# A two-layer graph network on one core: 64 more edge tiles counted, one-source compares for the one-hots, and fewer signals from TensorE

## The chip, the cores and the metric

The kernel runs on one core of a Trainium2 chip. Its time is the device time of one execution in microseconds; the number compared is the median of several runs. Engines are named as in the profile: PE is TensorE (matrix products), PEld its weight loads, DVE is VectorE, ACT is ScalarE, POOL is GpSimd, SP is SyncE, which here only starts transfers. Each engine works through its own list of instructions in order; an instruction can wait for a semaphore that another engine raises.

## The reference, cut to what matters

There are 12,500 nodes with 32 features and 200,000 edges, sorted by their destination `dst`. Two layers follow each other, each added to `x`:

```python
h = relu(layernorm(x))
# layer 0: sum of the neighbours' rows
agg = segment_sum((h * rsqrt(max(out_deg, 1)))[src], dst, N)
x = x + (agg * rsqrt(max(in_deg, 1))) @ W + b
...
# layer 1: a small network on every edge, then the mean over a node's edges
msg = concat([h[dst], h[src] - h[dst]])             # h = relu(layernorm(x)) again
m = relu(relu(relu(msg @ W1 + b1) @ W2 + b2) @ W3 + b3) @ W4 + b4
x = x + segment_sum(m, dst, N) / max(count, 1)
```

So the rows of `src` have to be fetched by index (a gather) or counted, and the rows of `dst` are summed over a sorted list.

## The kernel before, in words

The edges are cut into tiles of 128 (1563 of them) and chunks of four tiles (391). Sums over destinations are products with one-hot matrices: a tile's rows are multiplied with a matrix that has a 1 where an edge belongs to a node of a window of 128, and windows move on by 32 nodes a chunk. One gather instruction of POOL (L211, in `gather`) fetches 128 rows by index; a chunk takes four of them.

**Stage 0** (0 to about 475 us): the layer norm, the degrees (one-hots L325, products L342), tables of rows written to DRAM, and the gathers of the first 64 chunks ("early").

**Stage 1**, the first layer (about 480 to 1960 us), has three kinds of chunks.
- The 64 early chunks are in SBUF already. `scale_rows` looks up each edge's factor (`sturned` L659, products L677, `mask` L684) and sums them (L706). One is started every `LATER` = 3 steps.
- The chunks 64 to 267 (up to `DIR` = 268) are gathered: four gathers `rows`, and two steps later `sum_rows` with four products into `ps_late` (L641).
- The last `ND` = 491 tiles, from chunk 268 on, are counted and not gathered. For each tile a matrix `oh` (edges by 98 × 13 columns: block of 128 nodes, place in the tile's window of 13 destinations) and a one-hot `lo` of the low seven bits of the source are made. Their product (`count_two`: two matmuls of 429 columns in a PSUM tile of two banks; `count_third`: one of 416; L789) says how often a source feeds a destination. ACT copies the counts to SBUF in two instructions (L791). After eight tiles, `multiply` multiplies the counts with a table of all nodes' rows, which stays in SBUF: 98 products of 104 columns (L738), spread over five of the next eight tiles, then a transpose and a placing product (L752, L757).

The one-hots `oh` are made for two tiles at once by a two-source compare (L726, 2574 columns): `keys` holds an edge's key for each third of the blocks, spread over the columns, against the column numbers `count_h`. It works two pairs ahead.

The order is written out by hand. A step of the loop at L807 issues the four gathers of one chunk, then about 2.4 count tiles (`slots`, L819), and with the first of these the one-hots of the next chunk, the running `scale_rows`, and the sums of the chunk gathered two steps before. `count_edges` is a generator, and one `next` is one tile.

**Stage 2**, the second layer (about 2010 to 4340 us): `NPAIR` = 196 steps, each for a pair of chunks. A step issues eight gathers `gj` (six buffers), the loads `ai` (L882) and `row` (L885) on SP for the step three later, and the stages of four pairs, at lags of 1, 3, 4 and 5 steps:
- `first` (L904): transposes of `gj` and one-hot products with `ai` into `p1`; ACT makes `h1` (L920).
- `second` (L923): four products with `w2s` (L930) into `p2`; ACT makes `h2` (L932).
- `third` (L934): sixteen products (L940) into `p3`; DVE makes `h3` (L943).
- `fourth` (L947): sixteen products of `h3` with the one-hots `hot` (made on DVE, L584) into the sums `ps`; every other step `add_messages` adds them to the accumulators (L558, L560) and now and then starts `finish_nodes` (the last product, L869, and the output).

`turn` makes the one-hots `turned` for the next pair's `first` (DVE, L892). The order of a step in before is gathers, loads, `finish_nodes`, then first, second, third, fourth as they were put in the list, each with the ACT or DVE instruction that reads its product right behind it. Each stage's products end with a signal of PE to that reader; PSUM buffers come from pools in turn (`p1` and `p3` two, `p2` one).

Of the kernel before, what the change touches and what calls it, by code (L numbers as in the profile page):

```python
# [8 lines left out]
F32 = mybir.dt.float32  # L9
BF16 = mybir.dt.bfloat16  # L10
F16 = mybir.dt.float16
# [46 lines left out]
LATER = 3  # L58
# [6 lines left out]
DIR = 268  # L65
# [19 lines left out]
def gnn_kernel(  # L85
# [59 lines left out]
    keys = early.tile([P, 3, ND + 1], F16, name="keys")  # L145
# [64 lines left out]
    def gather(tile_ap, table, col):  # L210
        nc.gpsimd.indirect_dma_start(  # L211
            out=tile_ap, out_offset=None, in_=table,
            in_offset=bass.IndirectOffsetOnAxis(ap=col, axis=0))
# [72 lines left out]
    with tc.tile_pool(name="deg", bufs=3) as hp, tc.tile_pool(  # L286
# [105 lines left out]
        base_ps = pp.tile([P, ND], F32, name="base_ps")  # L392
        nc.tensor.matmul(base_ps, ones, base_f, start=True, stop=True)
        drel = hp.tile([P, ND], F32, name="drel", bufs=1)
        nc.vector.tensor_tensor(drel, dst_i[:, DIR * TPC : NTR], base_ps, op=OP.subtract)
        nc.vector.tensor_reduce(bounds[:, 0:1], drel, AX.X, OP.min)
        nc.vector.tensor_reduce(bounds[:, 1:2], drel, AX.X, OP.max)
        key = hp.tile([P, ND], F32, name="key", bufs=1)
        nc.vector.scalar_tensor_tensor(
            key, hl[:, 0, DIR * TPC : NTR], float(WD), drel, op0=OP.mult, op1=OP.add)  # L400
        nc.vector.memset(keys[:, :, ND:], 0.0)
        for k in range(3):
            nc.vector.tensor_scalar(keys[:, k, :ND], key, float(-KW * k), None, op0=OP.add)
# [194 lines left out]
    with tc.tile_pool(name="e0", bufs=8) as sp, tc.tile_pool(name="nu", bufs=1) as np_, tc.tile_pool(  # L598
# [53 lines left out]
        def scale_rows(g):  # L652
# [4 lines left out]
            yield  # L657
            turned = sp.tile([PART, CHUNK], BF16, name="sturned", bufs=2)
            nc.vector.tensor_scalar(turned, row, part_s[:PART], None, op0=OP.is_equal)  # L659
            h = rows_early[:, g, :, :D]  # L660
            if g < RAW:
# [3 lines left out]
                nc.vector.tensor_sub(h, h, m[:, :, None].to_broadcast([P, TPC, D]))  # L665
                square = sp.tile([P, TPC, D], F32, name="raw_sq", bufs=2)
# [21 lines left out]
            if g < RAW:  # L688
# [4 lines left out]
                scaled, h, 0.0, w[:, :, None].to_broadcast([P, TPC, D]), op0=OP.max, op1=OP.mult)  # L693
            rows = sp.tile([P, TPC, D3], BF16, name="rows_scaled", bufs=2)
# [7 lines left out]
            yield  # L702

            total = ps[:D3, 1]
            for t in range(TPC):
                nc.tensor.matmul(  # L706
                    total, rows[:, t, :], hot[:, t // 2, :, t % 2], start=(t == 0), stop=(t == TPC - 1))
            adds.append((g, total))
# [8 lines left out]
        los, onehots, counts = {}, {}, {}  # L717
        LATE = (TD - 3, TD - 2)

        def onehots_of(i):  # L720

            if i % TPC == 0:
                c = DIR * TPC + i
                los[i // TPC] = one_hots(dp, hl[:, 1, c : c + TPC], P, "lo", 3)
            onehots[i // 2] = oh = dp.tile([P, 3, KW, 2], BF16, name="oh", bufs=4)
            nc.vector.tensor_tensor(  # L726
                oh, keys[:, :, i : i + 2][:, :, None, :].to_broadcast([P, 3, KW, 2]),
                count_h[:, None, :, :].to_broadcast([P, 3, KW, 2]), op=OP.is_equal)
# [35 lines left out]
        def count_edges():  # L764
# [3 lines left out]
            onehots_of(0)  # L768
            onehots_of(2)
            for i in range(ND):  # L770
# [7 lines left out]
                if i % 2 == 0 and i + 4 < ND:  # L778
                    onehots_of(i + 4)
                oh, lo = onehots[i // 2], los[i // TPC]  # L780
                if t not in LATE:
                    next(before, None)

                for ranges, name in ((THIRDS[:2], "two"), (THIRDS[2:], "third")):
                    k0, a, b = THIRDS.index(ranges[0]), ranges[0][0], ranges[-1][1]
                    ps = pp.tile([P, len(ranges), 512], F32, name=f"count_{name}")
                    w = (b - a) // len(ranges) * WD
                    for k in range(len(ranges)):
                        nc.tensor.matmul(  # L789
                            ps[:, k, :w], lo[:, i % TPC // 2, :, i % 2], oh[:, k0 + k, :w, i % 2], start=True, stop=True)  # L790
                    nc.scalar.activation(  # L791
                        counts[g][:, t, a:b, :].rearrange("p (k h) d -> p k (h d)", k=len(ranges)), ps[:, :, :w], AF.Copy)
# [14 lines left out]
        for m in range(EARLY, DIR + LAG + 1):  # L807
# [3 lines left out]

            while adds:
                early, total = adds.pop()
                sums.add(slice(0, D3), STEP * early, total)
                added([early])
            if EARLY <= m - LAG - 1:
                add_rows(m - LAG - 1)
            i = m - EARLY
            slots = range(stages * i // steps, stages * (i + 1) // steps)  # L819
            for slot in slots:  # L820
# [335 lines left out]
```

## Time and profile before

| | |
|---|---|
| median of 10 runs | 4344.57 us (4329.93 to 4361.16) |
| the profiled execution | 4349.91 us |
| its span, first to last instruction | 4347.8 us (2.1 us lie around it) |
| mean granted clock of TensorE | 0.737 |

The costliest groups, as busy time and mean of one:

| what | how many | mean ns | busy us |
|---|---|---|---|
| POOL gathers `gj`, stage 2 (L211) | 1563 | 946 | 1478.2 |
| POOL gathers `rows`, stage 1 (L211) | 816 | 946 | 772.2 |
| PE third's products (L940) | 3128 | 322 | 513.8 |
| PE products with the table (L738) | 6076 | 226 | 424.2 |
| PE count products, two (L789) | 982 | 417 | 324.0 |
| ACT copies of the counts, two (L791) | 491 | 886 | 435.2 |
| ACT copies of the counts, third (L791) | 491 | 513 | 251.8 |
| DVE one-hots of two count tiles (L726) | 246 | 1488 | 365.6 |

The durations of PE's products overlap, since products are pipelined. The views used below are the page with the shares of the span, the same by stretch of the span ("windows"), the groups of instructions by line, the list of waits (engine and instruction, what ended the wait, total us, number, longest) and the order of time (start, duration, engine, line, output and inputs, and in brackets the engine's idle time before it with what ended it: "remote" is a releaser that the profile can't name, "issue" is idle time in which the engine waited for nothing that the profile shows).

### The profile page before, as it was taken

The page shows a single profiled execution, that of the slowest core. Times are in us where ns is not written, and L with a number is a line of the kernel's source. Part 1 is how long each engine was busy: PE and PEld are TensorE (multiplying, and loading weights), DVE is VectorE, ACT ScalarE, POOL GpSimd, SP SyncE. Part 2 cuts the span into 40 slices and gives each one's busy share as a digit, 9 for nine tenths or more (in the row PEclk, how much of TensorE's full clock was granted, in tenths as well). Part 3 has the DMA queues.
Part 4 walks back from the last instruction along what each step waited for, and adds up shares of the span by engine and source line. Part 5 has one row for each costly group of instructions (what it writes and reads, how often), then busy time and mean ns, then how long its engine had stood idle before and what let it go on. Part 6 is the DMA issues. An engine that isn't in the chain of part 4 may idle for free.

```text
span 4347.8 us, 54122 instructions
## 1 busy us (share of the span) xinstructions
PE 2909.2 (67%) x20860; PEld 1948.3 (45%) x20860; DVE 1821.0 (42%) x4113; ACT 1108.1 (25%) x2034; POOL 2501.6 (58%) x2655
## 2 busy tenths in 40 slices
PE   2444276777777777763667676777777777777777
PEld 2333154555555555551344444444444444444445
DVE  6555465666556566541222232222323222232224
ACT  0000244455544455430111111111111111111112
POOL 6555355555555555445566666666666666666663
PEclk9555588888888888865676777767767777667778
DMA  3000211111111111111222222222222222222221
GB/s 77 11 11 10 60 20 19 24 22 27 24 24 24 20 25 30 21 37 36 45 50 51 51 50 52 51 51 51 50 51 53 51 51 51 50 50 54 47 54 32
DMA packets 234664, 170.64 MB, mean 39 GB/s; under 512 B 156040, under 2 KB 182888, under 8 KB 234400
## 3 DMA queue, kind: packets, MB, share of 16 engines
q0 software_dynamic: 84320, 75.96, 11.0%
q1 hardware_dynamic: 131338, 85.26, 7.3%
q10 hardware_dynamic: 18742, 5.89, 0.7%
q8 instruction: 168, 2.75, 0.3%
q14 instruction: 96, 0.79, 0.1%
HBM read 153.98 MB, written 12.92 MB: 38 GB/s over the span
## 4 chain that ended last, share of the span: by engine, by line
PE 41%; another core or an unknown queue 19%; issue 16%; DVE 9%; ACT 8%; POOL 6%; DMA 1%; DVEq 0%; ACTq 0%; POOLq 0%
PE p L940 8%; PE p L930 6%; ACT count L791 6%; POOL gj L211 5%; PE count_two L789 4%; PE ps L958 4%; PE st L738 4%; PE p L916 4%; PE p L912 3%; DVE lo L325 2%; POOL rows L211 2%; PE count_third L789 2%; DVE hi L325 1%; PE ps_late L641 1%
## 5 line engine op out<-in xcount | busy, mean ns | idle before, releaser
L211 POOL DMA_INDIRECT gj<-tab_j,src_j x1563 | 1478.2, 946 | 904.3 <-issue 417.3
L211 POOL DMA_INDIRECT rows<-tab_hn,src_j x816 | 772.2, 946 | 747.4 <-PE ps_late L641 386.2
L940 PE MATMUL p<-w3s,h 128*128 128x64 f32 x3128 | 513.8, 322 | 177.6 <-issue 131.3
L943 DVE TENSOR_TENSOR h<-p,b3n 128x512 f32<-128x512 f32 x196 | 135.3, 690 | 1110.2 <-remote 491.1
L791 ACT ACTIVATE count<-count_two 128x858 bf16<-128x858 f32 x491 | 435.2, 886 | 624.9 <-remote 263.4
L940 PEld LDWEIGHTS p<-w3s,h 128*128 128x128 f32 x3128 | 473.3, 234 | 224.0 <-issue 166.7
L932 ACT ACTIVATE h<-p,b2s 128x1024 f32<-128x1024 f32 x196 | 218.0, 1112 | 1216.1 <-remote 546.9
L789 PE MATMUL count_two<-oh,lo 128*128 128x429 bf16 x982 | 324.0, 417 | 293.8 <-ACT count L791 239.6
L738 PE MATMUL st<-count,table 128*128 128x104 bf16 (+1 forms) x6076 | 424.2, 226 | 115.4 <-issue 72.0
L738 PEld LDWEIGHTS <-table 128*128 128x128 bf16 x6076 | 380.7, 105 | 180.3 <-issue 138.1
L930 PE MATMUL p<-h,w2s 64*128 64x512 f32 x782 | 383.1, 866 | 106.0 <-issue 87.9
L726 DVE TENSOR_TENSOR oh<-keys,kept 128x2574 bf16<-128x2574 f16 x246 | 365.6, 1488 | 54.3 <-PE ps_late L641 19.9
L958 PEld LDWEIGHTS ps<-hot,h 128*64 128x64 f32 x3126 | 233.9, 170 | 303.0 <-issue 152.4
L958 PE MATMUL ps<-hot,h 128*64 128x128 f32 x3126 | 269.7, 326 | 130.3 <-DVE h L943 129.4
L789 PEld LDWEIGHTS <-lo 128*128 128x128 bf16 x1473 | 150.8, 110 | 417.2 <-issue 368.9
L916 PE MATMUL p<-turned,ai 128*64 128x512 f32 x782 | 309.2, 837 | 20.0 <-issue 19.5
L342 PE MATMUL deg_ps<-hi,lo 128*128 128x98 bf16 x1563 | 182.8, 269 | 197.6 <-issue 132.5
L211 POOL DMA_INDIRECT rows_early<-tab_h,src_j x224 | 211.8, 946 | 157.9 <-DVE src_j L334 90.9
L912 PE MATMUL p<-ident,gj 128*128 128x128 f32 x784 | 195.2, 365 | 113.9 <-issue 113.4
L560 DVE TENSOR_TENSOR acc<-acc,ps 64x64 f32<-64x64 f32 (+1 forms) x198 | 44.6, 225 | 536.1 <-PE p L912 259.6
L892 DVE TENSOR_TENSOR turned<-row,kept 128x512 f32<-128x512 f16 x391 | 249.6, 679 | 33.8 <-remote 15.8
L791 ACT ACTIVATE count<-count_third 128x416 bf16<-128x416 f32 x491 | 251.8, 513 | 5.7 <-PE count_two L789 3.8
(201 smaller groups left out, 2918.1 us busy)
## 6 DMA issues: line engine op xcount, KB each, us to landing
row<-rel_row SPq DMA_DIRECT2D x195, 256.0 KB
gj<-tab_j,src_j POOLq DMA_INDIRECT x1563
rows<-tab_hn,src_j POOLq DMA_INDIRECT x816
ai<-tab_i SPq DMA_DIRECT2D x195, 64.0 KB
srow<-hi_row SPq DMA_DIRECT2D x64, 98.0 KB
rows_early<-tab_h,src_j POOLq DMA_INDIRECT x224
tab_j<-nu_aij SPq DMA_DIRECT2D x23, 128.0 KB
tab_i<-nu_aij SPq DMA_DIRECT2D x23, 128.0 KB
```

Of the source, the lines that this page charges most:

```text
L211: nc.gpsimd.indirect_dma_start(out=tile_ap, out_offset=None, in_=table, in_offset=bass.IndirectOffsetOnAxis(ap=col, axis=0))
L726: nc.vector.tensor_tensor(oh, keys[:, :, i : i + 2][:, :, None, :].to_broadcast([P, 3, KW, 2]), count_h[:, None, :, :].to_broadcast([P, 3, ...
L738: nc.tensor.matmul(ps[:, : tiles * WD], table[:, h, :], c[:, :tiles, h, :], start=(h == 0), stop=(h == PART - 1))
L789: nc.tensor.matmul(ps[:, k, :w], lo[:, i % TPC // 2, :, i % 2], oh[:, k0 + k, :w, i % 2], start=True, stop=True)
L791: nc.scalar.activation(counts[g][:, t, a:b, :].rearrange("p (k h) d -> p k (h d)", k=len(ranges)), ps[:, :, :w], AF.Copy)
L892: nc.vector.tensor_tensor(turned, v["row"][:, k], part_f.to_broadcast([P, CHUNK]), op=OP.is_equal)
L912: nc.tensor.matmul(p1[:, t, :], v["gj"][:, t].rearrange("p k c -> p (k c)"), ident, is_transpose=True, start=(t == 0), stop=False, skip_gr ...
L916: nc.tensor.matmul(p1[k * HID : (k + 1) * HID].rearrange("p t e -> p (t e)"), v["ai"][:, k], v["turned"][k], start=False, stop=True, skip_ ...
L930: nc.tensor.matmul(p2[:, k], w2s[s, :], v["h1"][s, :], start=True, stop=True)
L932: nc.scalar.activation(h2[:, :n], p2[:, :n], AF.Relu, bias=b2s)
L940: nc.tensor.matmul(p3[:, k * TPC + t, :], v["h2"][:, k, t * P : (t + 1) * P], w3s, start=True, stop=True)
L958: nc.tensor.matmul(ps[k * HID : (k + 1) * HID, o : o + W], v["h3"][:, k * TPC + t, :], v["hot"][k][:, t, :], start=(i == 0 and t == 0), st ...
```

## The change

It has three parts.

**Less is gathered, more is counted.** `DIR` goes from 268 to 252, so that 188 chunks are gathered in stage 1 (before 204), and 555 tiles are counted (before 491). A step has about three count tiles instead of 2.4. `scale_rows` is started every eighth slot and no more every third step, with more `yield`s in it, and the sums and the running generators are advanced in every slot.

**How a tile is counted.** The one-hots are made for one tile at a time, four tiles ahead, in seven buffers, by a one-source compare (`tensor_scalar`) of the column numbers `count_s` with the edge's key, which is a scalar of each partition. The two PSUM tiles of the counts are made once. The third product is split in 8 and 408 columns. Both of ACT's copies are made to wait for the tile's last product, so that PE raises its semaphore once a tile and no more twice.

**The order of stage 2.** In a step PE does fourth, third and first, then the products of `finish_nodes`, then second; the lags are 1, 2, 4 and 6. All instructions that read products (`past_first`, `past_second`, ...) come after second, in the lists of ACT and DVE. `ends[step]` is second's last product; h3's instruction, the gathers (of the step five later) and the `ai` loads are made to wait for it (`behind`), and with the in-order lists this stands for the signals of the other stages. PSUM buffers are fixed tiles.

The instructions that the programs hold, before and after: signals of PE in stage 2's stages 881 and about 206; signals of PE by count products 982 and 555, by all of stage 1 1588 and 1226; products by the count tiles 1473 and 2220; products with the table 6076 and 6860; gathers of `rows` 816 and 752.

```diff
-LATER = 3
+LATER = 8
-DIR = 268
+DIR = 252
...
-    keys = early.tile([P, 3, ND + 1], F16, name="keys")
+    key = early.tile([P, ND], F32, name="key")
+    count_s = early.tile([P, 3 * KW], F16, name="count_s")
...
         for k in range(3):
-            nc.vector.tensor_scalar(keys[:, k, :ND], key, float(-KW * k), None, op0=OP.add)
+            nc.vector.tensor_scalar(
+                count_s[:, KW * k : KW * (k + 1)], count_h[:, :, 0], float(KW * k), None, op0=OP.add)
...
+        count_ps = {name: pp.tile([P, n, 512], F32, name=f"count_{name}") for name, n in (("two", 2), ("third", 1))}
+        FIRST = 8
+        AHEAD_OH = 4
...
-            onehots[i // 2] = oh = dp.tile([P, 3, KW, 2], BF16, name="oh", bufs=4)
-            nc.vector.tensor_tensor(
-                oh, keys[:, :, i : i + 2][:, :, None, :].to_broadcast([P, 3, KW, 2]),
-                count_h[:, None, :, :].to_broadcast([P, 3, KW, 2]), op=OP.is_equal)
+            onehots[i] = oh = dp.tile([P, 3 * KW], BF16, name="oh", bufs=7)
+            nc.vector.tensor_scalar(oh, count_s, key[:, i : i + 1], None, op0=OP.is_equal)
...
+                        for c in (slice(0, w),) if name == "two" else (slice(0, FIRST), slice(FIRST, w)):
+                            o = KW * (k0 + k)
+                            end = nc.tensor.matmul(
+                                ps[:, k, c], lo[:, i % TPC // 2, :, i % 2], oh[:, o + c.start : o + c.stop], start=True,
+                                stop=True, skip_group_check=True)
+                    copies.append((counts[g][:, t, a:b, :].rearrange("p (k h) d -> p k (h d)", k=len(ranges)), ps[:, :, :w]))
+
+                for to, of in copies:
+                    tc.add_manual_dep(
+                        nc.scalar.activation(to, of, AF.Copy).ins, end.ins.name,
+                        mybir.DependencyInfo(mybir.DependencyClass.Sync, mybir.DependencyReason.DATA))
...
+            for slot in slots:
+                while adds:
+                    early, total = adds.pop()
+                    sums.add(slice(0, D3), STEP * early, total)
+                    added([early])
+                if slot == slots[0] and EARLY <= m - LAG - 1:
+                    add_rows(m - LAG - 1)
...
+                later, r = divmod(slot - 3, LATER)
+                if r == 0 and later < EARLY:
+                    running.append(scale_rows(later))
+                advance(running)
...
+        firsts = [pp1.tile([P, TPC, P], F32, name=f"p1_{k}") for k in range(2)]
+        thirds = [pp2.tile([P, 2 * TPC, HID], F32, name=f"p3_{k}") for k in range(2)]
+        whole = pp2.tile([P, 2, CHUNK], F32, name="p2")
...
+        ends = {}
+        def behind(r, step):
+            if step in ends:
+                tc.add_manual_dep(
+                    r.ins, ends[step].ins.name,
+                    mybir.DependencyInfo(mybir.DependencyClass.Sync, mybir.DependencyReason.DATA))
...
+            behind(r, m - AHEAD - 2)
...
+                    behind(gather(gj[:, t, k, :], tab_j[:, :], src_j[:, c : c + 1]), m - 5)
...
+                ends[step] = nc.tensor.matmul(p2[:, k], w2s[s, :], v["h1"][s, :], start=True, stop=True)
...
+            behind(nc.vector.tensor_tensor(
+                h3[:, :n], v["p3"][:, :n], b3n[:, None, :].to_broadcast([P, n, HID]), op=OP.max), step)
...
+            for stage, lag in ((first, 1), (second, 2), (third, 4), (fourth, 6)):
...
+            order = [(m, stage) for stage in (fourth, third, first) for m, s in now if s is stage]
+            for m, stage in order:
+                stage(m)
             advance(running)
-            for k, stage in now:
-                stage(k)
...
+            seconds = [m for m, s in now if s is second]
+            for m in seconds:
+                second(m)
+            for m in seconds:
+                past_second(m)
+            for stage in (first, third, fourth):
+                for m, s in order:
+                    if s is stage:
+                        past[stage](m)
+            if step + 1 < NPAIR:
+                turn(step + 1)
```

## The prediction

> **What bounds it now.** Look first at the busy shares of the page, then at the stages (busy time of each engine in a stretch of the span).
>
> ```profile
> PE 2909.2 (67%) x20860; PEld 1948.3 (45%) x20860; DVE 1821.0 (42%) x4113; ACT 1108.1 (25%) x2034; POOL 2501.6 (58%) x2655
> ```
> ```profile
> 1200.00:1800.00 600.00, 436.79 (x4327) 327.97 (x4325) 362.58 (x997) 304.23 (x587) 316.58 (x335) 0.85 0.15 24
> 2700.00:3300.00 600.00, 435.06 (x2373) 267.43 (x2374) 176.79 (x349) 99.97 (x166) 381.09 (x403) 0.71 0.23 51
> ```
>
> The columns after the length are busy us (and instructions) of PE, PEld, DVE, ACT and POOL, then PE's granted clock. No engine is full in either stage, so the engines wait for each other. A count tile of stage 1 goes from its first product at 498.3 to the last at 1900.4: 1402/491 = 2.86 us per tile, or 1420/204 = 6.96 us per gathered chunk. Stage 2 takes some 2330 us for 196 steps, 11.9 us each. The waits say who waits for whom:
>
> ```profile
> POOL rows L211 <- PE ps_late L641: 386.2, 116, 7.8
> POOL gj L211 <- PE p L912: 238.6, 62, 7.3
> ACT count L791 <- remote: 265.2, 79, 8.4
> ```
>
> POOL waits for PE to free the row buffers, and ACT waits for something that the profile can't name ("remote"). The order of time around 1200 us shows what that is:
>
> ```profile
> 1198.70 0.55 PE L789 MATMUL count_two<-oh,lo 128*128 128x429 bf16 x2 [1.04 <-ACT count L791]
> ...
> 1200.85 0.95 POOL L211 DMA_INDIRECT rows<-tab_hn,src_j  x1 [0.30 <-issue]
> 1201.09 0.38 DVE L748 TENSOR_SCALAR place<-kept,pos 104x160 f32<-104x160 f16 x1
> 1202.89 0.89 ACT L791 ACTIVATE count<-count_two 128x858 bf16<-128x858 f32 x1 [3.83 <-remote]
> 1203.68 0.51 ACT L791 ACTIVATE count<-count_third 128x416 bf16<-128x416 f32 x1
> 1203.83 0.87 PE L789 MATMUL count_two<-oh,lo 128*128 128x429 bf16 x2 [3.33 <-ACT count L791]
> ```
>
> PE's two products end at 1199.25, ACT has been idle since 1199.06, and yet ACT's copy starts at 1202.89, 1.1 us after POOL's last gather of that row ended (1201.80). PE then waits 3.33 us for the copy. I compared the end of each PE instruction that raises its semaphore with the trace's semaphore events: with POOL idle for over 2.5 us fewer than 1% of PE's signals come more than 0.5 us late; from the third gather in a row on 75% do, by 1.7 to 2 us on average. So **in a run of gathers few of PE's signals get through**: per 4-gather burst, some 2.7 in its 5 us, and as many in the one microsecond after. POOL's own release comes that way too, hence its pause of typically 1.45 us after four gathers and 2.0 us after eight.
>
> Stage 2 has a second form of it. After about 125 PE instructions (91 to 171) within one burst, each further one takes 0.7 us:
>
> ```profile
> 3010.56 0.34 PE L940 MATMUL p<-w3s,h 128*128 128x64 f32 x2 [0.86 <-issue]
> ...
> 3011.29 0.22 PE L940 MATMUL p<-w3s,h 128*128 128x64 f32 x1 [0.38 <-issue]
> ...
> 3012.01 0.22 PE L940 MATMUL p<-w3s,h 128*128 128x64 f32 x1 [0.51 <-issue]
> ...
> 3022.85 0.69 DVE L943 TENSOR_TENSOR h<-p,b3n 128x512 f32<-128x512 f32 x1 [15.60 <-remote]
> ...
> 3023.81 0.94 POOL L211 DMA_INDIRECT gj<-tab_j,src_j  x1 [4.00 <-PE p L912]
> ```
>
> Between 2600 and 3400 us there are 32 bursts of 8 gathers (11.7 us from one to the next, never slow) and 18 of 16 (24.3 us for two steps, some 10 us of them slow): (32 × 11.7 + 18 × 24.3)/68 = 11.9 us per step.
>
> **The change, part by part.**
>
> *Fewer gathers.* 16 chunks leave the gathered part: 64 gathers of 1.25 us each (946 ns and 0.30 of issue), 80 us of POOL's time, and their sums (64 products of 0.25 us). They come back as 64 more counted tiles. A tile that nothing stalls takes 1.5 to 1.8 us, so these add about 64 × 1.65 = 106 us. That alone, with 16 pauses fewer (48 us at most, 3 us of stall each), is +58 to +106.
>
> *The one-hots.* The rows:
>
> ```profile
> L726 DVE TENSOR_TENSOR oh<-keys,kept 128x2574 bf16<-128x2574 f16 x246 | 365.6, 1488 | 54.3 <-PE ps_late L641 19.9 <-PE count_third L789 16.3 <-remote 10.0
> L659 DVE TENSOR_SCALAR sturned<-srow,part_s 98x512 bf16<-98x512 f16 x64 | 22.9, 357 | 20.0 <-DMA srow<-hi_row 16.5 <-issue 3.5
> ```
>
> Now 1488/2 = 744 ns a tile. The new form (one source, 1287 columns) isn't in the trace; L659 is the nearest: 512 columns in 357 ns. If 133 ns of these are columns (four a cycle) 1287 take 224 + 335 = 0.56 us; if two a cycle, 0.89. I take 0.56 (same types and form as L659). 555 of them are 311 us, or 494 at the other end, against 366. DVE is 60% busy there and works four tiles ahead; even 494 leaves it under 75%, so this is worth nothing directly.
>
> POOL's side of it: gathers that ran beside an L659 lasted 953 ns on the mean against 946, 1.05 us at most. So 7 ns, at most 105, for each gather touched: about 5 us of POOL time, and POOL has slack. The Trainium skill speaks against the change here ("SBUF — State Buffer", section "A bandwidth-pool intuition that's wrong"): a fast one-source VectorE operation holds a port that GpSimd needs to write descriptors, so that a transfer of 620 ns took 3100. By that rule POOL would stand still for 0.56 us a tile, a chunk would cost POOL 4.7 + 2.95 × 0.56 + 1.45 = 7.8 us, and stage 1 would be 47 us longer than now, instead of shorter. The row says otherwise, and I go by the row.
>
> *One signal a tile.* PE's signals in stage 1 fall from 1588 to 1226 by the built programs: from 3.2 to 2.2 per tile. What that is worth: a chunk takes 4.7 us of gathers, and the tiles that don't get their signals through in it come after. Before, 2.7/3.2 = 0.84 tiles get through, of 2.41 a chunk: 4.7 + 1.57w = 6.96 gives w = 1.44 us. After, 2.7/2.2 = 1.23 of 555/188 = 2.95: 4.7 + 1.72 × 1.44 = 7.18 us. Against it: both copies now wait for the third product. ACT's loop was 1.52 us from copy to copy and becomes about 1.77 (three products at 0.19 us apart before the first copy), +0.25 where ACT binds; I let it bind for half of the 1.72 tiles: +0.2. So 7.3 to 7.4 us × 188 = 1380, against 1420: **−40 to −50 us**. Bounds: never below POOL's own loop of 6.15 us (4.7 + 1.45) × 188 = 1156, −260; never above the tiles' own cost with the ACT loop, 58 + 53 = +111.
>
> *Smaller pieces of stage 1.* The split third product adds 555 products of 8 columns (nearest row: 128x8 in 175 ns, much of it overlapped): 0.05 to 0.17 us a tile on an engine that waits; inside the numbers above. Yields in the scaled rows only spread the same work over more slots. The set-up's extra product and subtraction: under 2 us.
>
> *Stage 2.* Signals fall from 881 to about 206 (4.5 to 1.05 a step); instructions stay at 98.6 a step, gathers at 8. POOL is still five to six steps ahead at most: before, a buffer of six freed by `first`; now `ends[m-5]`, the end of the step in which that same `first` ran, some 3 us later in the step. The new waits: h3 on DVE waits for the end of `second`; behind it stand hot, turned and the sums, all of the same step, and PE needs h3 two steps later. ACT's h2 (1.11 us) and h1 (0.6) come after the same signal, and `second` needs both one step later, behind fourth, third and first (some 6 us of PE). So a signal may be about 5 us late before PE stops: that is what hides the change, and each us above 5 costs 196 us over all. The ai transfers wait on SP for the step before last; behind them are the row transfers, needed two steps (23 us) later: nothing. With one signal instead of five in the queue I expect the pause after eight gathers to be that of stage 1, 1.45 us instead of 2.0; the share of bursts of 16 stays, since instructions per gather stay: (32 × 11.15 + 18 × 24.3)/68 = 11.68, −0.26 × 196 = **−50 us**. Bounds: POOL without a pause, 10.0 × 196, −370; all bursts of 16, +265 (below).
>
> **Sum.** 4349.9 − 45 − 50 = 4255 for the profiled execution (span 4347.8 and 2.1 around it); the median of the runs is 5 lower, so 4250.
>
> **Rivals.**
> A, stage 2 comes free. If the stalls there come from late signals more than from the slow 0.7 us steps, a step falls to 10.0 to 10.5 us (POOL's 8 × 1.25 and little pause): 196 × 10.5 = 2058, −270, with stage 1 about 4030, down to 3930. For it: DVE's 15.6 us and ACT's 9.6 us of waiting in the stretch above. Against it: PE itself was slow there. Chance 0.18.
> B, slower: with one signal a step POOL finds its release always there and gathers 16 at a time. PE gets its 125 instructions and then 0.7 us each for the other 19 to 54 of two steps: 19.7 + 2.2 + 2 to 4.5 = 23.8 to 26.4 per two steps, 12 to 13.2 a step. At 13.2: +265, with stage 1 about 4560. It decides from 12.2 us a step on. For it: the 18 bursts of 16. Against it: 32 of 50 bursts stopped at 8. Chance 0.20.
> C, the signals aren't what stalls counting (gathers hold the tiles up for another reason, or four gathers always cost one stall whatever the count): the change doesn't do what it says, the tiles cost +58 to +111, stage 2 stays: 4400 to 4455. Chance 0.17.
>
> **Numbers.** The forecast has 0.45, its own range 4170 to 4340. About 0.3% (13 us) is what a measurement of this kernel can tell from no change. Faster: A's 0.18 and 0.39 of the forecast's; same: 0.06; slower: B, C, less what of them falls near zero, 0.37. The range reaches from 4020, in the middle of A, to 4450, which takes C in and leaves out most of B.
>
> **What would show it.** Right: a counted chunk near 7.3 us and fewer "remote" waits of ACT; one-hots near 0.56 us and gathers still at 946 ns; pauses of POOL near 1.45 us in stage 2 and a step at 11.4 to 11.9. Wrong: gathers over 1.1 us (the port), a chunk over 7.6 us (C), PE's 0.7 us steps taking more than the 490 us of stage 2 now (B), or a step under 11 (A).

## The result, and the profile after

The changed kernel takes 4650.87 us (median of 9 runs, 4627.18 to 4661.07), the kernel before 4346.1 (31 runs): 1.0686 times as long, 95% interval 1.0665 to 1.0706. The prediction was 4250, faster, with a range from 4020 to 4450; the kernel became 305 us slower.

Three differences between the two profiled executions make up the 294.5 us between their spans (4642.3 and 4347.8). The first gather of the second layer starts at 2058.9 instead of 1982.0: **+77**. From the first to the last of these gathers it takes 2543.3 instead of 2340.2, 13.0 us a step instead of 12.0: **+203**. From the start of the last one to the end it takes 40.1 instead of 25.6: **+15**. That part, too, goes with the order of PE in a step: the runs below whose first product in a step is fourth's have 40 to 43 there, those with fourth behind first 28 to 31, although fourth comes six steps behind its gathers in both. (One with fourth at the head but the sums issued earlier, adds_first, has 28.7.)

The page, and the same two stretches as before (busy us and instructions of PE, PEld, DVE, ACT, POOL, then the granted clock):

```profile
PE 3037.2 (65%) x22353; PEld 2076.9 (45%) x22353; DVE 1745.8 (38%) x4444; ACT 1177.7 (25%) x2173; POOL 2466.6 (53%) x2591
```
```profile
1200.00:1800.00 600.00, 453.74 (x4651) 347.24 (x4650) 318.15 (x1115) 315.53 (x604) 280.43 (x285) 0.84 0.13 22
2700.00:3300.00 600.00, 399.71 (x2170) 249.10 (x2168) 159.18 (x313) 86.64 (x148) 349.60 (x372) 0.70 0.20 47
```

In the first layer PE and ACT do more in the same time, POOL less. In the second layer everything does less: 350 us of gathers in 600 instead of 381. So the engines wait more, and the list of waits of the changed kernel (engine and instruction, what it waited for, us, times, longest) has names for it:

```profile
ACT h L976 <- PE p L970: 1255.5, 103, 15.7
DVE h L990 <- PE p L970: 1105.3, 103, 14.3
...
POOL rows L212 <- PE ps_late L644: 620.7, 174, 8.2
...
POOL gj L212 <- PE p L970: 504.7, 91, 7.7
PE ps L1005 <- ACT acc L561: 500.3, 74, 8.6
...
ACT count L811 <- PE count_third L804: 311.9, 355, 4.3
PE count_two L804 <- ACT count L811: 294.0, 248, 8.2
...
PE ps L1005 <- DVE acc L563: 66.4, 10, 8.3
```

L970 is second's last product, the one signal of a step: ACT, DVE and POOL all wait for it now. New are the rows of L1005: PE, at the first product of fourth, waits for ACT's copy into the accumulators or for DVE's addition to them. In order of time:

```profile
3013.36 1.13 PE L970 MATMUL p<-h,w2s 64*128 64x512 f32 x4
...
3016.59 0.94 POOL L212 DMA_INDIRECT gj<-tab_j,src_j  x1 [0.30 <-issue]
...
3019.42 0.69 DVE L990 TENSOR_TENSOR h<-p,b3n 128x512 f32<-128x512 f32 x1 [8.73 <-remote]
...
3019.76 1.11 ACT L976 ACTIVATE h<-p,b2s 128x1024 f32<-128x1024 f32 x1 [10.49 <-remote]
...
3020.77 0.59 ACT L963 ACTIVATE h<-p 128x512 f32<-128x512 f32 x1
...
3021.46 0.27 ACT L561 ACTIVATE acc<-ps 64x128 f32<-64x128 f32 x1
3021.76 0.22 DVE L563 TENSOR_TENSOR acc<-acc,ps 64x64 f32<-64x64 f32 x1 [0.34 <-ACT acc L561]
...
3022.02 0.27 ACT L561 ACTIVATE acc<-ps 64x128 f32<-64x128 f32 x1 [0.29 <-DVE acc L563]
...
3022.35 1.98 PE L1005 MATMUL ps<-hot,h 128*64 128x128 f32 x16 [7.86 <-ACT acc L561]
```

PE ends a step at 3014.49. The signal arrives at 3019.4, 1.9 us after the last gather of POOL's run has ended (3017.53); then come h2, h1, copy, addition, copy, 2.9 us, and only then fourth of the next group may start: PE has stood still for 7.86 us. The waits of L1005 for ACT and DVE come to 84 in 98 groups, a group being two steps. By the trace, 96 of its waits are over 2 us, 646 us together, and every one ends 52 to 57 ns after the last copy or addition of such sums. The program says why: the first product of a new group waits for the sums of the group just before it. The two halves of `both` lie in one PSUM tile, and fourth, formerly the last stage of a step, is now the first one after the sums were issued.

**Two conditions.** The same kernels ran on chips at two levels: the kernel before took 3376 to 3379 us in three of the five sets of runs below, and 4307 to 4346 in the other two and in the runs above (two of the chips showed both levels). At 3376 none of PE's signals is late (s2_only, whose first layer is that of the kernel before: 0 of 1369 by over 0.5 us, with POOL in a run of gathers at 98% of them), and POOL's gathers set the second layer at 9.98 us a step. I call the two "prompt" and "late". The names stand for one sign of several: at 3376 PE's 0.7 us instructions are all but gone too (30 intervals of 0.6 to 0.8 us between the starts of successive PE or PEld instructions in s2_only from 1450 to 3340 us, with POOL gathering on end; 467 in the kernel before from 2150 to 4250), and the first layer's gathers start at 339 us and not at 490. What makes the difference isn't known. Only late runs speak of this result; the prompt ones show what the change costs when lateness plays no part.

### The profile page after: what moved, and what is told of

It is laid out like the page before. It is cut to its first block, busy times and chain, and to the rows that moved or that the text cites. A ratio compares the mean times of both kernels' runs of the same rounds, so it can differ in the third digit from the quotient of the medians.

```text
span 4642.3 us, 57476 instructions
## 1 busy us (share of the span) xinstructions
PE 3037.2 (65%) x22353; PEld 2076.9 (45%) x22353; DVE 1745.8 (38%) x4444; ACT 1177.7 (25%) x2173; POOL 2466.6 (53%) x2591
## 4 chain that ended last, share of the span: by engine, by line
PE 43%; another core or an unknown queue 24%; ACT 13%; issue 10%; DVE 8%; ACTq 1%; DMA 0%; DVEq 0%
PE p L983 8%; ACT count L811 7%; PE p L955 5%; PE count_two L804 5%; PE st L749 5%; PE ps L1005 5%; PE p L970 4%; PE count_third L804 3%; PE p L951 3%; ACT h L976 3%; DVE lo L326 2%; DVE hot L587 1%; DVE hi L326 1%; ACT h L963 1%
## 5 line engine op out<-in xcount | busy, mean ns | idle before, releaser
L1005 PE MATMUL ps<-hot,h 128*64 128x128 f32 x3126 | 305.5, 354 | 654.8 <-ACT acc L561 500.3
L811 ACT ACTIVATE count<-count_two 128x858 bf16<-128x858 f32 x555 | 491.4, 885 | 646.3 <-PE count_third L804 311.9
L1005 PEld LDWEIGHTS ps<-hot,h 128*64 128x64 f32 x3126 | 240.3, 181 | 852.9 <-ACT acc L561 618.7
L983 PE MATMUL p<-w3s,h 128*128 128x64 f32 x3128 | 561.1, 354 | 8.6 <-issue 8.6
L983 PEld LDWEIGHTS p<-w3s,h 128*128 128x128 f32 x3128 | 529.4, 263 | 60.0 <-issue 60.0
L749 PE MATMUL st<-count,table 128*128 128x104 bf16 (+1 forms) x6860 | 471.5, 226 | 62.5 <-issue 51.9
L804 PEld LDWEIGHTS <-lo 128*128 128x128 bf16 x2220 | 229.6, 110 | 547.8 <-issue 457.7
L749 PEld LDWEIGHTS <-table 128*128 128x128 bf16 x6860 | 427.5, 105 | 87.2 <-issue 76.8
L955 PE MATMUL p<-turned,ai 128*64 128x512 f32 x782 | 351.9, 854 | 52.0 <-issue 51.9
L739 DVE TENSOR_SCALAR oh<-count_s,key 128x1287 bf16<-128x1287 f16 x555 | 308.9, 564 | 50.7 <-remote 25.0
L970 PE MATMUL p<-h,w2s 64*128 64x512 f32 x782 | 287.8, 810 | 33.2 <-ACT h L976 31.2
L587 DVE TENSOR_TENSOR hot<-rel_h,kept 128x512 f32<-128x512 f16 x391 | 249.1, 678 | 0.0
```

The lines of the kernel that those rows point to most:

```text
L587: nc.vector.tensor_tensor(hot, rel_h[:, g * TPC : (g + 1) * TPC][:, :, None].to_broadcast([P, TPC, W]), lanes_f[:, None, :W].to_broadcast( ...
L739: nc.vector.tensor_scalar(oh, count_s, key[:, i : i + 1], None, op0=OP.is_equal)
L749: nc.tensor.matmul(ps[:, : tiles * WD], table[:, h, :], c[:, :tiles, h, :], start=(h == 0), stop=(h == PART - 1))
L804: end = nc.tensor.matmul(ps[:, k, c], lo[:, i % TPC // 2, :, i % 2], oh[:, o + c.start : o + c.stop], start=True, stop=True, skip_group_ch ...
L811: nc.scalar.activation(to, of, AF.Copy).ins, end.ins.name,
L955: nc.tensor.matmul(p1[k * HID : (k + 1) * HID].rearrange("p t e -> p (t e)"), v["ai"][:, k], v["turned"][k], start=False, stop=True, skip_ ...
```

## The experiments

Theory 1: in the second layer, fourth at the head of a step waits for sums that can only follow the step's single, late signal; in the first, the wait of both copies for the last product lengthens ACT's loop. Rivals: theory 2, which is the prediction's rival B (runs of 16 gathers starve PE), and theory 3 (everything waits for one late signal, whatever PE does first).

A step in the table is the time from the first to the last gather of the second layer, divided by its 195.4 steps.

| run | signals | before, us | ratio (95%) | first layer's gathers, first to last | step |
|---|---|---|---|---|---|
| before (profile) | late | 4346 | 1 | 1449 (204 chunks, 7.10 each) | 11.98 |
| changed (profile) | late | 4346 | 1.0686 (1.0665–1.0706) | 1541 (188, 8.20) | 13.02 |
| s1_only | prompt | 3377 | 1.0266 (1.0246–1.0286) | 1124 (5.98) | 9.98 |
| s2_only | prompt | 3377 | 1.0047 (1.0031–1.0064) | 1026 (5.03) | 9.99 |
| fourth_last | prompt | 3377 | 1.0295 (1.0275–1.0314) | 1128 (6.00) | 9.99 |
| adds_first | prompt | 3377 | 1.0270 (1.0252–1.0289) | 1143 (6.08) | 9.98 |
| after_again | prompt | 3379 | 1.0311 (1.0275–1.0346) | 1124 (5.98) | 9.99 |
| two_signals | prompt | 3379 | 1.0054 (1.0035–1.0074) | 1042 (5.54) | 9.98 |
| dir268 | prompt | 3379 | 1.0092 (1.0062–1.0121) | 1056 (5.18) | 9.99 |
| two_signals_fourth_last | late | 4307 | 1.0093 (1.0051–1.0135) | 1452 (7.72) | 12.10 |
| lead2 | prompt | 3376 | 1.0011 (1.0001–1.0022) | 1042 (5.54) | 9.99 |
| lead2_s1_before | prompt | 3376 | 1.0021 (1.0011–1.0032) | 1022 (5.01) | 9.99 |
| fourth_last_d | late | 4314 | 1.0174 (1.0128–1.0220) | 1492 (7.94) | 11.98 |
| lead2_s1_before_b | late | 4314 | 1.0014 (0.9999–1.0030) | 1430 (7.01) | 11.94 |

Three repeats ran prompt too and told nothing new: fourth_last_b 1.0274, after_c 1.0322, fourth_last_c 1.0277.

**One layer of the change at a time.** Two kernels, each with one layer of the changed kernel and the other of the kernel before.

> The changed first layer (252 chunks' border, one-source one-hots, one signal a counted tile) with the second layer as before. The traces of before and after put the first gather of the second layer at 1982.0 and 2058.9 us. If the two parts don't act on each other, this is 77 us slower than before: about 4422. If the second layer alone is the loss (the first layer's shift being made good by a shorter second layer, or a chance of one profile), it is within 20 us of before.

> The first layer as before with the changed second layer. The traces put 203 us between the lengths of the second layer's gathers and 14 us more behind the last gather: about 4345 + 217 = 4562 if the parts are independent. If the longer time came from the first layer's larger number of instructions or tiles, it stays below 4450.

Both ran prompt. The first layer costs 88 us there, the second 17, mostly the longer tail. So the first layer loses by itself, without late signals; and the second layer's 203 us don't show without them, as long as POOL gathers at 9.98 us a step and PE needs less in either order.

**The order of PE in a step.**

```diff
-            order = [(m, stage) for stage in (fourth, third, first) for m, s in now if s is stage]
+            order = [(m, stage) for stage in (third, first, fourth) for m, s in now if s is stage]
```

> The changed kernel, with one edit: in a step of the second layer TensorE does third, first, fourth and then second, instead of fourth, third, first and second. Theory 1 (the first product of fourth, at the head of a step, waits for the sums of the group before, which come only after the late last signal of the step before; 588 us of waits of that product stand in the list): the wait is covered by third and first, about 6 us of TensorE, so most of 6 us in two steps goes: 400 to 550 us less, 4100 to 4250. Theory 2 (the one signal a step lets POOL run 16 gathers on end, and TensorE gets no instructions): the order changes nothing of that, 4600 to 4660. Theory 3 (whatever TensorE does first, everything waits for the same late signal): a gain of less than 100 us, since second then waits for h1 in place of fourth.

Prompt, so it told nothing of the theories. The same edit was run again in fourth_last_d, with late signals:

> The changed kernel with third, first, fourth, second as its only edit. The kernel before beside it tells whether signals are late there (4300 to 4350) or not (3375). If late: 12.0 to 12.1 us a step in the second layer where the changed kernel had 13.0; if the other edit had a hand in it, near 13. If not late: 9.98.

Late this time: 11.98 us a step, and 2340.5 us from the first to the last gather, where the kernel before had 2340.2 and the changed one 2543.3. With this edit the loss of the second layer is gone. The stretch from 2500 to 3500 us in the kernel before, the changed one and fourth_last_d, and the waits of L1005 in the last:

```profile
2500.00:3500.00 1000.00, 721.92 (x3952) 443.07 (x3952) 293.24 (x578) 165.43 (x273) 636.74 (x674) 0.72 0.23 51
```
```profile
2500.00:3500.00 1000.00, 672.70 (x3614) 418.38 (x3614) 267.30 (x528) 145.36 (x250) 581.05 (x616) 0.69 0.20 47
```
```profile
2500.00:3500.00 1000.00, 733.43 (x3968) 459.44 (x3967) 291.62 (x578) 158.78 (x272) 640.99 (x679) 0.72 0.21 51
```
```profile
PE ps L1005 <- issue: 355.4, 388, 2.3
...
PE ps L1005 <- ACT acc L561: 123.5, 49, 4.9
```

POOL's gathers are back at 641 us in 1000, and fourth's waits for ACT's copies fall from 500.3 to 123.5 us. In time it is 1.0174 against 1.0686, some 220 us, less than the 400 to 550 first expected: what PE no longer waits, it loses in part again in 0.7 us instructions (554 intervals of 0.6 to 0.8 us between 2150 and 4250, 387 us of them; 300 and 210 us in the changed kernel). Not all of the difference is the edit's: the changed kernel was met late in the first measurement alone, and its first layer, which the edit leaves as it is, took 1541 us there and 1492 here. The pair without gathers below compares the two orders on one chip.

**The sums ahead of h2, h1 and h3.** `past_fourth` is called first after the end of a step.

> The changed kernel, with one edit: behind the end of a step, the sums of fourth stand first in the lists of ACT and DVE, ahead of h2, h1, h3 and the one-hots. Theory 1: the chain from the signal to fourth was 2.9 us (h2 1.11, h1 0.6, a copy, an addition, a copy); it falls to about 1.2, so 1.7 us in two steps, 98 times: 165 us less, about 4485. Theory 2: no change. Theory 3: no change or a loss, h1 and h2 being later by 0.8 us.

It ran only prompt (1.027, as without the edit); what it is worth with late signals is open.

**The second layer without gathers.** POOL is taken out: plain transfers bring fixed rows, which leaves out the fetching by index.

```diff
-                for t in range(min(TPC, NTR - g * TPC)):
-                    c = g * TPC + t
-                    behind(gather(gj[:, t, k, :], tab_j[:, :], src_j[:, c : c + 1]), m - 5)
+                n, r = min(TPC, NTR - g * TPC), CHUNK * (g % 24)
+                behind(nc.sync.dma_start(
+                    gj[:, :n, k, :], tab_j[r : r + P * n, :].rearrange("(p t) c -> p t c", t=n)), m - 5)
```

> The kernel before, with the second layer's gathers by index left out: each chunk's rows come by one plain transfer of SP from a fixed place of the table (so the output is not that of the reference). POOL is idle there, so no signal should be late and no run of gathers starves TensorE. It shows what a step costs when only the order of the engines counts: between TensorE's own work (some 7.5 to 8.5 us a step, by its busy time) and POOL's former 10.0. If steps of 10 us or more stay, something other than POOL sets them.

> The changed kernel with the same gathers left out. Theory 1 (fourth at the head of a step waits for the sums of the group before, which follow the step's last signal): without lateness the chain of 2.9 us stays, once in two steps, so a step is 1.2 to 1.5 us longer than with fourth behind first, and the first product of fourth waits for ACT's copies 98 times. Theory 2 (long runs of gathers starve TensorE): without gathers nothing is lost, the step is that of the kernel before or shorter. Theory 3 (some other wait on the one signal): longer than before, and not mended by the order.

> The same, with TensorE's order third, first, fourth and then second. Theory 1: a step 1.2 to 1.5 us shorter than in the changed order, and no waits of fourth for the sums. Theories 2 and 3: the same within 0.3 us a step.

They ran where signals are late (the kernel before took 4307 there): in the first layer of plain_after 47% of the signals raised in a run of gathers were late; in its second layer, with POOL idle, 0 of 208. One execution each: 3105.5, 3825.5 and 3151.4 us; a step took 5.79, 9.30 and 5.71 us. So the order alone costs 3.6 us a step, where 1.2 to 1.5 were expected. The same stretch (2500 to 3000 us) of plain_after and then plain_fourth_last tells where the rest comes from; the last three numbers are PE's clock, the DMA share and GB/s:

```profile
2500.00:3000.00 500.00, 418.89 (x2535) 268.78 (x2533) 187.34 (x371) 102.01 (x176) 0.00 (x0) 0.78 0.26 65
```
```profile
2500.00:3000.00 500.00, 500.00 (x4112) 343.76 (x4113) 303.48 (x600) 165.34 (x286) 0.00 (x0) 1.00 0.44 106
```

PE is never idle in the second, at full clock; in the first it has a clock of 0.78. In order of time in plain_after:

```profile
2500.12 1.13 PE L970 MATMUL p<-h,w2s 64*128 64x512 f32 x4
...
2504.22 1.09 PE L1005 MATMUL ps<-hot,h 128*64 128x128 f32 x16 [2.98 <-ACT acc L561]
...
2505.24 3.09 PE L983 MATMUL p<-w3s,h 128*128 128x64 f32 x16
...
2509.44 1.97 PE L955 MATMUL p<-turned,ai 128*64 128x512 f32 x4
...
2514.10 2.00 PE L983 MATMUL p<-w3s,h 128*128 128x64 f32 x16
...
2516.75 1.08 PE L955 MATMUL p<-turned,ai 128*64 128x512 f32 x4
```

The wait is the 2.98 us of the chain. But after it the third takes 3.09 us, and 2.00 in the next step; first's four products 1.97, and 1.08. The windows put numbers to it (start to end, length, PE's busy time, ..., clock):

```profile
2501.00:2504.00 3.00, 0.24 (x2) 0.00 (x0) 2.34 (x6) 1.98 (x4) 0.00 (x0) 1.00 0.25 77
2504.00:2508.00 4.00, 3.78 (x32) 3.61 (x32) 1.18 (x2) 0.17 (x1) 0.00 (x0) 0.74 0.43 94
2508.00:2512.00 4.00, 4.00 (x14) 1.75 (x15) 0.00 (x0) 0.00 (x0) 0.00 (x0) 0.50 0.00 0
2512.00:2516.00 4.00, 4.00 (x36) 2.71 (x32) 2.80 (x5) 1.60 (x2) 0.00 (x0) 0.91 0.24 61
```

So a pause of 3 us is followed by half the clock. It is so each time: from 2200 to 3500 us there are 70 such pauses (2.97 to 3.09 us) and 70 stretches at 0.50, each of 6.8 or 10.2 us, 587 us together. Two steps are 7.2 us longer than with the other order (9.30 − 5.71, twice): 3.0 of waiting, which leaves 4.2. The slow clock accounts for that: 587/70 = 8.4 us at half the clock for two steps are 4.2 us lost, as an estimate for a PE that is busy throughout. That is theory 1 with a multiplier that its expectation lacked. Theory 2 is out for this part, there being no gathers; theory 3 too, since the order mends it. The Trainium skill ("TensorE: Matmul & The Clock Gate", section "HAM oscillation — how this bites in real kernels") warns of idle gaps above about 3.4 us on PE; here 2.98 us were enough.

**The first layer: one signal or two a tile.** ACT's first copy waits for its own two products again.

```diff
-                copies = []
...
-                    copies.append((counts[g][:, t, a:b, :].rearrange("p (k h) d -> p k (h d)", k=len(ranges)), ps[:, :, :w]))
-
-                for to, of in copies:
-                    tc.add_manual_dep(
-                        nc.scalar.activation(to, of, AF.Copy).ins, end.ins.name,
-                        mybir.DependencyInfo(mybir.DependencyClass.Sync, mybir.DependencyReason.DATA))
+                    nc.scalar.activation(
+                        counts[g][:, t, a:b, :].rearrange("p (k h) d -> p k (h d)", k=len(ranges)), ps[:, :, :w], AF.Copy)
```

> The changed kernel without an edit, beside the kernel before on the same chip. The last four kernels ran on a chip where the kernel before took 3377 us (its signals are not late there: 0 of 1369 in the first layer by over 0.5 us), against 4345 for the runs that the prediction is about. If a chip like the first is met: 4650, with the first layer's gathers over 8.2 us a chunk and the second layer's 13.0 us a step. On one like the last: 3475, with 6.0 and 9.98.

> The changed kernel, with ACT's first copy of a counted tile waiting for its own two products, as before, and no more for the tile's last one: two signals of TensorE a tile. If the single signal is what costs the first layer its time (copies start later, ACT's loop 1.77 against 1.52 us), a tile is 0.2 us faster: 60 to 110 us less. If one signal is a gain where signals are late, 30 to 90 us more there, and the same or less where they are not.

> The changed kernel with both edits: ACT's first copy waits for its own two products, and fourth stands behind first. Where signals are late: 60 to 110 us less from the first layer and 400 to 550 less from the second, 4000 to 4200, faster than the kernel before. Where they are not: 3390 to 3400, as with the first edit alone, since POOL's gathers set the second layer.

Prompt, beside after_again: 3395.6 against 3482.3, 87 us less, 82 of them in the first layer (1042 against 1124). What ACT waits for, between 600 and 1300 us, in after_again and then in two_signals:

```profile
ACT count L811 <- PE count_third L804: 187.8, 309, 4.1
...
PE count_two L804 <- ACT count L811: 90.8, 120, 1.2
```
```profile
ACT count L806 <- PE count_two L803: 130.1, 208, 2.4
...
PE count_two L803 <- ACT count L806: 73.0, 132, 1.2
```

ACT's waiting falls by 58 us in 700 and PE's by 18. Late, with both edits: 1452 us for the first layer, where the changed one had 1499 and 1505 in the two plain kernels on the same chip, and the kernel before 1429 there. So there the change costs this layer 70 to 76 us (92 on the chip of the first measurement); the second signal gives back 47 to 54 of them, and all that the change still costs, 64 more tiles included, is 23. The single signal is a loss under either condition. With both edits the kernel stands at 1.0093.

**The number of counted tiles**, with DIR = 268 and LATER = 7:

> The changed kernel with the border of chunks back at 268 (491 counted tiles, 204 gathered chunks; LATER is 7, so that all early chunks are done in the fewer slots). If the first layer's loss is the 64 tiles, at 1.8 to 2.7 us each, most of it goes: 75 to 100 us less than the changed kernel. If it is a slower tile, whatever their number, about 10 to 40 less.

Prompt: 74 us less than the changed kernel, just below the 75 to 100 of the first expectation. With late signals it was not run. In the changed kernel the tiles set the pace: 555 at 2.02 us are 1119 of the layer's 1124 us. 491 would take 990, but with 204 chunks POOL sets the pace again, 204 × 5.18 = 1056 us; in the kernel before it was 5.03 a chunk. The groups of gathers of dir268 and of s2_only (whose first layer is that of the kernel before) have the reason:

```profile
L212 POOL DMA_INDIRECT rows<-tab_hn,src_j x816 | 809.0, 991 | 248.7 <-issue 178.0 <-DMA rows<-tab_hn,src_j 43.6 <-PE count_third L804 13.1
```
```profile
L211 POOL DMA_INDIRECT rows<-tab_hn,src_j x816 | 771.0, 945 | 256.7 <-issue 188.3 <-DMA rows<-tab_hn,src_j 35.0 <-PE ps_late L641 11.7
```

A gather takes 46 ns longer on the mean: four to a chunk, 0.18 us. It goes with the one-source compares: in dir268 the gathers that start within one last 1050 ns, those that touch none 944, and in s2_only the gathers that start within a two-source compare last 944.

**Shorter runs of gathers.** Both edits above, and the gathers wait for the end of the step two before (`m - 2` in place of `m - 5`); in lead2_s1_before_b the first layer is that of the kernel before.

> Both edits (fourth behind first; two signals a counted tile), and the gathers of a step wait for the end of the step two before, not five before, so that POOL can't run 16 gathers on end. Rival B (long runs starve TensorE of instructions and hold its signals) says for late signals: bursts of 8 only, 9.7 + 1.45 to 2.0 of pause, 11.2 to 11.7 us a step, 60 to 160 us less than with 12.09. If the runs of 16 cost nothing, because POOL makes up in them what it loses elsewhere: 12 us or more, no gain, since POOL now waits for the late signal in every step. Where signals are not late: 10.0, no difference.

> The first layer as before, third, first, fourth, second, and gathers two steps behind. Rival B, if signals are late: bursts of 8 only, 11.2 to 11.7 us a step, 50 to 150 less than the kernel before. If runs of 16 are not what holds a step at 12 us: 12 or more, and no gain. If not late: 3384 once more.

Late, 1.0014 (0.9999 to 1.0030): the same time as the kernel before, 11.94 us a step. But the edit didn't do what it was meant to: between 2150 and 4250 us there were still 53 runs of 16 (before: 45) beside 69 of 8, a pause of under 0.7 us counted as part of a run. It says nothing against runs of 16 as the reason why a step takes 12 us with late signals; that part of rival B stays open. No kernel here that fetches by index beats the kernel before under either condition.

## Why the prediction was wrong

**"−50 for stage 2" failed at the step where its waits were priced.** The prediction listed h3, hot, turned, h2 and h1 behind the new single signal, found 5 us of PE work in front of each, and concluded that a signal may be 5 us late before PE stops. It named the sums of `past_fourth` among them ("all of the same step") and didn't ask when PE needs them. Fourth, now at the head of the next step, needs them at once: the cover is zero. The runs put the whole +203 us there: with fourth behind first, the stretch is 2340.5 us long. In the changed kernel 93 of the 196 step ends had a signal late by over 0.5 us, by 4.9 us on the mean, 67 of them by no more than the 5 us that the prediction counted on. In the example above PE stood still for 7.9 us, 4.9 of them until the signal came and 2.9 for the chain behind it. Nor does "each us above 5 costs 196 us" come out: the wait falls once in two steps, and 646 us of it made the stretch 203 us longer, partly in place of other losses (PE's 0.7 us instructions fell from 328 to 210 us); where the rest went isn't worked out.

**"The pause will be 1.45 us instead of 2.0" failed too.** Where the order is mended, PE raises one signal a step and POOL's pause after eight gathers still has a median of 1.94 us (2.03 before), and a step 11.98. Fewer signals bought nothing there, which speaks against a pause made of signals that are worked off one by one.

**"−45 for stage 1": two terms.** The gain from fewer signals rested on a quota, some 2.7 of them getting through a burst whatever their number. In the changed kernel some 2.0 reach their engines in a 4-gather burst, 0.9 tiles at 2.2 a tile, against 0.84 before and the 1.23 that the sum took; of those raised during a run in this layer, about half were late in both (50 and 49%). That fits a share set by time within the run better than a fixed number. An estimate with the prediction's own terms says as much: with 0.84 tiles through, as before, a chunk takes 4.7 + 2.11 × 1.44 + 0.2 = 7.94 us, 72 us over the sum's 1420 for the layer; 7.94 to 8.01 was measured in fourth_last_d and the two plain kernels, 8.20 in the changed one. The loss from the later copies was in the sum as +0.2 us a chunk (some 38 us) and measured 47 to 54 us over the layer with late signals, 82 with prompt ones. Rival C had the failed step ("the signals aren't what stalls counting"), at +58 to +111 us and 0.17, and the layer came out at 92. That its number holds is in part luck: the most of it was the later copies, and what was left for the tiles (23 us) is less than its lower end. The sum also started too low: the gathers that it put at 1420 us take 1449 from first to last, 7.10 us a chunk.

**Rival B's price, not its mechanism.** Its 4560 (its +265 should be 255 by its own 13.2 and 11.9 us) lies nearer to 4651 than anything else in the prediction. Runs of 16 did become a little more frequent, 50 between 2150 and 4250 us against 45. But fourth_last_d has 53 and the step of the kernel before, and PE's 0.7 us instructions, which B made the cost, fell from 328 us to 210. What grew was POOL's gap after a run of 16, from 3.7 to 7.1 us (medians): its release is the end of a step, and PE reaches that later by its wait for the sums.

**Right:** the compares (564 ns against 560 predicted; the upper price of 0.89 us should have been 0.76 by the prediction's own reading, 90 ns of L659's 357 being left if 267 are columns); that PE's signals, where they are late, are so with POOL's gathers (0 of 208 late without them), though the prompt runs show that gathers alone don't make them late; the ai loads on SP (no engine waits for them). **Under-priced:** gathers beside the compares, 7 ns predicted for each that is touched. Measured are 1029 ns for the 371 that overlap one, 1058 for the 213 that start within one, 944 for those that touch none, and 39 ns more on the mean of all (985 against 946):

```profile
L739 DVE TENSOR_SCALAR oh<-count_s,key 128x1287 bf16<-128x1287 f16 x555 | 308.9, 564 | 50.7 <-remote 25.0 <-PE count_third L804 20.9 <-issue 4.2
```
```profile
L212 POOL DMA_INDIRECT rows<-tab_hn,src_j x752 | 741.0, 985 | 866.1 <-PE ps_late L644 620.7 <-issue 176.4 <-PE c_ps L454 64.9
```

The rule of the Trainium skill that the prediction weighed ("SBUF — State Buffer", section "A bandwidth-pool intuition that's wrong (but worth ruling out)") was right that POOL is held up, which the row of L659 (7 ns) hardly showed; the size was 39 ns a gather on the mean, far from a whole compare for each. It decides nothing here, where POOL waits for PE anyway; in dir268, where POOL is the bound, it is 0.15 us a chunk, some 30 us.

## What to carry to other kernels

When many signals are folded into one, list everything that stands behind the one that is left, down to the last instruction of each queue, and look up who needs it first: the stage that was moved to the head of the step is the one without cover. A wait on TensorE is to be priced with the clock behind it: here 3.0 us of waiting cost 7.2. And a model in which "so many get through" fits one trace as well as "so much time is open" should be kept with both readings, because they part as soon as the number is changed.

## What the runs showed of the hardware that was not expected

- The same program and chip number can run with PE's signals prompt during POOL's gathers (0% late by over 0.5 us, 3376 us) or late (in the first layer 47 to 50% of those raised during a run, by 1.4 to 1.8 us on the mean from its third gather on; 4307 to 4346 us). What decides it isn't known; the gathers last 945 ns in both.
- Each of 70 pauses of TensorE of 2.97 to 3.09 us brought the granted clock from 1.00 to 0.50, for 6.8 or 10.2 us. Without gathers and pauses (plain_before, plain_fourth_last) it stayed at 1.00 throughout the second layer.
- A one-source compare of 1287 columns (564 ns) lengthens the gathers that start in it from 944 to 1058 ns on the mean, at most to 2.58 us; a two-source compare of 2574 columns (1488 ns) does not (944 and 945 ns).
